# New constants in the ledger that paces an involution under an attention (VectorE and GpSimd charged by start-to-start intervals)

## The chip, the cores and the metric

The kernel runs on one core of one Trainium2 chip. The metric is the device time of one execution, in microseconds (us); lower is better. Engines are named as in the profile: PE (TensorE matmul), PEld (its weight loads), DVE (VectorE), ACT (ScalarE), POOL (GpSimd) and SP (the queue that issues most transfers).

## The reference

Four images x of 512 channels by 64 x 64 pixels in fp32 go through two layers.

```python
# layer 0: attention over the 4096 pixels of one image, 128 inner channels
q, k, v = wq @ xf + bq, wk @ xf + bk, wv @ xf + bv
attn = softmax(einsum('bci,bcj->bij', q, k), axis=-1)
x = wo @ einsum('bcj,bij->bci', v, attn) + bo + x
# layer 1: involution, 7 x 7 taps, 8 groups of 16 channels
o = relu(affine(W1 @ x))                  # 512 -> 128 channels
w = Ws @ relu(affine(Wr @ o)) + bs        # 49 x 8 weights for every pixel
out[g, c, h, w] = sum over taps of w[g, tap] * o_padded[g, c, shifted by tap]
x = affine(W3 @ out) + x                  # 128 -> 512 channels
```

The softmax is taken without a running maximum. A second, general path in the program runs only if a check on the row sums asks for it; it does not run on these inputs.

## The kernel before, in words

**Attention.** An image's 4096 pixels are eight chunks of 512. `keys_values` (L473) makes keys and values of an image, chunk by chunk. `attention` (L647) then goes through the query chunks; a chunk has 32 steps. A step m issues the score matmul `pss` of step m + 2, ACT's exponential into `pt` (five buffers), the output matmul `po` of step m, and DVE's addition of `pt` into `pacc`, whose column sums give the softmax's divisor. Each 512-column product is two instructions on PE. The last image's last chunk is done as two halves of 256 queries.

**Finishing a chunk.** `finish_block` (L520) is a generator with the rest of a chunk: the row sums (`blocks`, `pl`, `rls`, `spread`), the normalised output `on`, four `pwo` matmuls and updates of `x`, the 512-to-128 product `p`, its result `o`, a transpose of it that goes by DMA into a padded image in DRAM (`pix`), and the reduced channels `red`. A chunk holds two involution units; `units` lists those whose chunk is finished.

**Involution.** A unit is four image rows; an image has 16, numbered 0 to 15. `ring` holds windows of `pix` rows in SBUF, loaded by `pump` (L240) through SP. `involution` (L306) makes, per unit, the tap weights `pw` on PE (into a PSUM bank that the unit before has read), and then products `prod<-ring,pw` on DVE (L356), each over three or four tap lines (one or two where the ring wraps): 49 lines in 14 to 21 products. The first product of the unit goes straight into `acc`; the others go through four `prod` buffers and are added to `acc` by POOL (L380). Two folds on POOL (L389) end the unit. In the first three images `turn_unit` (L395) then transposes the unit with DVE (`turned`, L404) and DMAs (`turns`, `accT`); in the last image PE transposes it (L436). `close_chunk` (L454) makes four `py` matmuls, DVE's updates of `x`, and the store.

**What sets the order.** All this is written into one program in an order that a ledger decides while the program is built; no engine reads it at run time. `pe` is the time of all matmuls issued so far (0.86 us for 512 columns). `free["dve"]`, `free["pool"]` and `free["dma"]` say until when those are taken; `takes` (L176) books an operation:

```python
def takes(engine, us):
    free[engine] = max(free[engine], pe) + us
    return free[engine]
```

After some of its matmuls the attention calls `chores` (L269): one step of a finishing block, one of a closing, and `pace` (L232), which lets `involution` go on while it has credit (1.56 tap lines per us of `pe`, at most 20). A product is issued only when this does not hold:

```python
while not tail and (
    pe < max(begin, landed)
    or free["dve"] > pe + (4.5 if b == B - 1 else 3.5)
    or free["pool"] > pe + lag
):
    yield "wait"
free["pool"] = max(free["pool"], takes("dve", DVE_TAPS[0] + DVE_TAPS[1] * n))
takes("pool", POOL_TAPS[0] + POOL_TAPS[1] * n)
```

`lag` is 4.0 us while keys and values are made and 7.5 in the attention. The POOL line is booked for every product, the first of a unit too, for which POOL gets nothing. `DVE_OP` is booked for each addition of `pt` (L692) and for the 512-column steps of finishing and closing (L403, L460, L536 to L559, L603); 1.5 `POOL_OP` for a unit's two folds (L392). A unit begins when `pe` has reached `free["dve"]` + 0.3 (L313). `turn_unit` waits for POOL's booked end + 2.0; in the last image the finishing block waits twice for `free["dve"]` + 0.8 (`HOP_US`).

**The tail.** When the last image's attention is written, `tail` is set. From then on no wait of the ledger holds, and every second product of a unit is summed on PE, by multiplication with the identity (`pa<-ident,prod`), instead of on POOL.

A scheduler behind the program may reorder instructions on an engine; products inside the attention are pinned to their place.

Of the kernel before, what the change touches and what calls it, by code (L numbers as in the profile page):

```python
# [64 lines left out]


PE_COLUMN = 0.43 / 256
DVE_OP, POOL_OP = 0.7, 1.28
DVE_TAPS, POOL_TAPS = (0.16, 0.27), (0.19, 0.55)
ROW_US, X_US, PIX_US, LAND_US = 2.2, 3.8, 1.5, 3.0  # L70
HOP_US = 0.8
STEP_US = 1.0
# [1052 lines left out]
```

## Time and profile before

| what | before |
|---|---|
| time, median of 3 runs (lowest to highest) | 2606.61 us (2604.79 to 2607.39) |
| span of the profiled execution | 2605.7 us |
| PE busy | 2587.9 us, 99% |
| DVE busy | 1874.2 us, 72% |
| POOL busy | 1823.5 us, 70% |
| ACT busy | 835.8 us, 32% |
| POOL additions (L380) | 1063, 1701.5 us |
| DVE products into `prod` (L356) | 1092, 886.7 us |
| DVE additions into `pacc` (L696) | 958, 664.6 us |
| granted PE clock, mean | 0.997 |

The profile is one execution. Its span runs from the first to the last instruction, and no time of the whole execution is given beside it, so it is the profiled execution's own time here, 0.9 us below the median of the runs. A group's "mean" is the time between an instruction's start and its end in the record; the distance from one start to the next is read from the timeline, which lists start, duration, engine, line, operation, output and inputs, shape, count, and in brackets how long the engine was idle before and who ended that. The chain of waits follows the last instruction back to what released it. PE's instructions overlap, so that its rate too is read from starts.

Inside the attention the four images are nearly copies of each other: units 1 to 15 of image 1 and of image 2 start at the same distances to within 0.1 us.

### The profile page before, as it was taken

How to read it: one execution, taken by the hardware profiler on the slowest of the kernel's cores; microseconds unless marked ns; L12 is line 12 of the kernel's file. 1: busy time of each engine (PE TensorE's matmuls, PEld its weight loads, DVE VectorE, ACT ScalarE, POOL GpSimd, SP SyncE). 2: the span in 40 equal slices, each digit the busy share in tenths (PEclk: the TensorE clock that was granted, in tenths of full speed). 3: DMA queues.
4: the chain of work that ended last, by engine and by line, in shares of the span. 5: the costliest groups of instructions: out<-in, count | busy, mean ns of one | idle time of the engine just before them, and what ended most of it. 6: DMA issues, size and time to landing. Idle time of an engine off the chain costs nothing.

```text
span 2605.7 us, 24569 instructions
## 1 busy us (share of the span) xinstructions
PE 2587.9 (99%) x7484; PEld 1246.5 (48%) x7484; DVE 1874.2 (72%) x2677; ACT 835.8 (32%) x1378; POOL 1823.5 (70%) x1197
## 2 busy tenths in 40 slices
PE   9999999999999999999999999999999999999998
PEld 7444444445544444444644444444464444444577
DVE  0447777877575787788676678788757678777887
ACT  1333333332233333333223333333323333333330
POOL 0007788877881788887885468888788577877886
PEclk9999999999999999999999999999999999999999
DMA  6033232445615344233651434443463433222343
GB/s 236 1 75 63 55 85 73 99 99 150 164 43 112 63 101 95 61 84 82 180 129 45 103 69 101 101 92 74 118 171 83 101 93 93 72 60 58 73 91 102
DMA packets 208798, 244.33 MB, mean 94 GB/s; under 512 B 109640, under 2 KB 128528, under 8 KB 208528
## 3 DMA queue, kind: packets, MB, share of 16 engines
q1 hardware_dynamic: 208224, 242.31, 38.6%
q8 instruction: 61, 1.00, 0.2%
q14 instruction: 81, 0.66, 0.1%
q10 hardware_dynamic: 432, 0.36, 0.0%
HBM read 193.57 MB, written 49.06 MB: 93 GB/s over the span
## 4 chain that ended last, share of the span: by engine, by line
PE 91%; POOL 4%; DVE 3%; issue 1%; DMA 0%; ACT 0%; SPq 0%; POOLq 0%; DVEq 0%; ACTq 0%
PE pss L220 32%; PE po L220 31%; PE pv L220 4%; PE pk L220 4%; PE pq L220 4%; PE pwo L220 4%; PE py L220 4%; PE p L220 4%; POOL acc L380 4%; PE pw L220 2%; DVE prod L356 1%; PE pa L220 1%; DVE pacc L696 1%; PE pr L220 1%; POOL acc L389 0%
## 5 line engine op out<-in xcount | busy, mean ns | idle before, releaser
L380 POOL TENSOR_TENSOR acc<-acc,prod 128x768 f32<-128x768 f32 (+3 forms) x1063 | 1701.5, 1620 | 760.5 <-DVE prod L356 712.4
L220 PE MATMUL pss<-q,k 128*128 128x512 f32 (+1 forms) x2112 | 1056.3, 585 | 0.0
L220 PE MATMUL po<-pt,v 128*128 128x512 f32 (+1 forms) x2112 | 1047.7, 581 | 0.0
L665 ACT ACTIVATE pt<-pss 128x512 f32<-128x512 f32 x1024 | 611.3, 597 | 1252.0 <-PE pss L220 1184.9
L356 DVE TENSOR_TENSOR prod<-ring,pw 128x512 f32<-128x512 f32 (+3 forms) x1092 | 886.7, 847 | 44.6 <-POOL acc L380 41.7
L696 DVE TENSOR_TENSOR pacc<-pacc,pt 128x512 f32<-128x512 f32 x958 | 664.6, 694 | 243.2 <-ACT pt L665 216.2
L220 PEld LDWEIGHTS po<-pt,v 128*128 128x128 f32 x2112 | 399.3, 190 | 482.2 <-issue 462.2
L220 PEld LDWEIGHTS pss<-q,k 128*128 128x128 f32 x2112 | 391.9, 190 | 466.2 <-issue 459.3
L404 DVE STREAM_TRANSPOSE turned<-acc 128x256 f32<-128x256 f32 x48 | 21.4, 446 | 217.4 <-POOL acc L389 217.4
L220 PE MATMUL py<-accT,wt 128*128 128x512 f32 (+1 forms) x264 | 132.3, 584 | 4.0 <-DVE x L461 3.3
L220 PE MATMUL pwo<-on,wt 128*128 128x512 f32 (+1 forms) x264 | 130.3, 586 | 0.0
L220 PEld LDWEIGHTS pv<-wt,x 128*128 128x128 f32 x1024 | 119.6, 192 | 15.3 <-issue 15.0
L389 POOL TENSOR_TENSOR acc<-acc 128x512 f32<-128x512 f32 x120 | 119.5, 996 | 9.4
L461 DVE SCALAR_TENSOR_TENSOR x<-py,vec,x 128x512 f32<-128x512 f32 (+1 forms) x132 | 95.7, 726 | 36.1 <-PE py L220 35.8
L220 PE MATMUL pv<-wt,x 128*128 128x128 f32 x1024 | 120.2, 275 | 0.0
L220 PE MATMUL p<-x,wt 128*128 128x512 f32 (+1 forms) x264 | 119.2, 579 | 0.0
L578 ACT ACTIVATE x<-x,vec 128x512 f32<-128x512 f32 (+1 forms) x132 | 92.9, 706 | 80.0 <-PE p L220 74.9
L220 PE MATMUL pk<-x,wt 128*128 128x512 f32 x256 | 117.3, 596 | 0.1
L220 PE MATMUL pq<-x,wt 128*128 128x512 f32 (+1 forms) x264 | 115.4, 580 | 0.0
L560 DVE SCALAR_TENSOR_TENSOR x<-pwo,bo,x 128x512 f32<-128x512 f32 (+1 forms) x132 | 95.2, 727 | 22.8 <-PE pwo L220 21.7
L356 DVE TENSOR_TENSOR acc<-ring,pw 128x1024 f32<-128x1024 f32 (+1 forms) x84 | 78.7, 955 | 17.6 <-PE pw L220 17.6
L220 PEld LDWEIGHTS pq<-x,wt 128*128 128x128 f32 x264 | 50.0, 190 | 60.2 <-issue 56.7
(57 smaller groups left out, 733.6 us busy)
## 6 DMA issues: line engine op xcount, KB each, us to landing
x<-x_dram SPq DMA_DIRECT2D x55, 1024.0 KB, 5.7
ring<-pix SPq DMA_DIRECT2D x74, 448.0 KB, 8.3
ring<-pix SPq DMA_DIRECT2D x24, 1344.0 KB, 9.7
out_dram<-x SPq DMA_DIRECT2D x31, 1024.0 KB, 4.2
ring<-pix SPq DMA_DIRECT2D x24, 896.0 KB, 10.7
ring<-pix SPq DMA_DIRECT2D x30, 672.0 KB, 10.2
ring<-pix SPq DMA_DIRECT2D x6, 2240.0 KB, 19.5
pix<-o1t SPq DMA_DIRECT2D x192, 32.0 KB, 1.7
```

The source lines that it names most:

```text
L220: return nc.tensor.matmul(o, lhsT=lhsT, rhs=rhs, start=start, stop=stop)
L356: product = nc.vector.tensor_tensor(prod[:, :, p0 : p0 + n, :].rearrange("p t d (g c) -> p t d g c", g=G), image.rearrange("p t d (g c) -> ...
L380: nc.gpsimd.tensor_tensor(acc[:, :, d0 : d0 + n, :], acc[:, :, d0 : d0 + n, :], prod[:, :, :n, :], ALU.add,)
L389: nc.gpsimd.tensor_tensor(acc[:, :, :n, :], acc[:, :, :n, :], acc[:, :, n : 2 * n, :], ALU.add)
L404: nc.vector.transpose(blocks.rearrange("p (t k q) -> p t k q", t=NT, q=TB), acc[:, :, 0, :].rearrange("p t (k q) -> p t k q", q=TB),)
L461: nc.vector.scalar_tensor_tensor(xt[:, t, :], py, v1(V_S3 + t), xt[:, t, :], ALU.mult, ALU.add)
L560: nc.vector.scalar_tensor_tensor(xt[:, t, :], pw, bo[:, t : t + 1], xt[:, t, :], ALU.add, ALU.add)
L578: nc.scalar.activation(xt[:, t, :], xt[:, t, :], AF.Identity, bias=v1(V_B3 + t))
L665: nc.scalar.activation(pt, pss, AF.Exp)
L696: nc.vector.tensor_tensor(paccs[k], paccs[k], pt, ALU.add)
```

## The change

Five numbers of the ledger are replaced. `DVE_OP` and `POOL_OP` are the booked time of a 512-element operation on DVE and POOL. `DVE_TAPS` and `POOL_TAPS` are a fixed part and a part per tap line of a product and of its addition. The old numbers are near an instruction's duration, the new ones are meant as the time from one instruction's start to the next one's.

```diff
 PE_COLUMN = 0.43 / 256
-DVE_OP, POOL_OP = 0.7, 1.28
-DVE_TAPS, POOL_TAPS = (0.16, 0.27), (0.19, 0.55)
+DVE_OP, POOL_OP = 0.62, 1.23
+DVE_TAPS, POOL_TAPS = (0.065, 0.267), (0.14, 0.545)
 ROW_US, X_US, PIX_US, LAND_US = 2.2, 3.8, 1.5, 3.0
```

| booked, us | before | after |
|---|---|---|
| DVE, product of 4 / 3 / 2 / 1 lines | 1.24 / 0.97 / 0.70 / 0.43 | 1.133 / 0.866 / 0.599 / 0.332 |
| POOL, addition of 4 / 3 / 2 / 1 lines | 2.39 / 1.84 / 1.29 / 0.74 | 2.32 / 1.775 / 1.23 / 0.685 |
| DVE, addition of `pt` | 0.70 | 0.62 |
| POOL, a unit's folds | 1.92 | 1.845 |

No instruction is written differently. What changes is after which matmul a product, a unit's weights, a finishing or a closing step stands in the program, and so how much of the last image is left when `tail` is set.

## The prediction

> **What bounds the kernel now.** I read the page's engine shares first, then stretches of the span, then the waits, then rows of the timeline.
>
> ```profile
> span 2605.7 us, 24569 instructions
> PE 2587.9 (99%) x7484; PEld 1246.5 (48%) x7484; DVE 1874.2 (72%) x2677; ACT 835.8 (32%) x1378; POOL 1823.5 (70%) x1197
> ```
>
> TensorE (PE) is busy for all but 17.8 us. The table of stretches (busy us of PE, weight loads, DVE, ACT, POOL; then the granted clock) shows where those lie:
>
> ```profile
> 694.00:1247.00 553.00, 551.70 (x1332) 239.13 (x1331) 425.34 (x620) 187.76 (x309) 404.61 (x270) 1.00 0.37 84
> 1959.00:2525.00 566.00, 565.99 (x1555) 275.60 (x1554) 441.03 (x630) 200.58 (x338) 432.76 (x287) 1.00 0.34 80
> 2525.00:2606.00 81.00, 68.00 (x460) 57.34 (x458) 64.55 (x92) 4.97 (x12) 52.66 (x33) 0.93 0.36 94
> ```
>
> Image 1 leaves PE idle 1.3 of 553 us, the last image's attention nothing, and the tail (attention over, the involution's rest alone) 13 of 81. An earlier product can shorten only the tail; inside the attention it can only remove or make stalls.
>
> The waits (us in total, times, longest) say who waits for the paced work:
>
> ```profile
> POOL acc L380 <- DVE prod L356: 712.4, 157, 199.8
> DVE turned L404 <- POOL acc L389: 217.4, 48, 7.3
> DVE prod L356 <- POOL acc L380: 41.7, 76, 1.8
> ACT pt L665 <- DVE prod L356: 39.0, 31, 2.0
> ```
>
> The transposes `turned` hold DVE 4.5 us each, at most 7.3, and PE does not stop behind any: ACT is late 2.0 us at most, and the score matmul that needs ACT's buffer still starts 1.78 us or more after ACT's end around each of them.
>
> **The change, part by part.** No instruction is added or dropped in the attention; five constants of a ledger change. So the first question is how each constant stands to start-to-start times. Back-to-back rows of DVE's timeline (start, duration):
>
> ```profile
> 1486.99 0.69 DVE L696 TENSOR_TENSOR pacc<-pacc,pt 128x512 f32<-128x512 f32 x1
> 1487.59 0.94 DVE L356 TENSOR_TENSOR prod<-ring,pw 128x768 f32<-128x768 f32 x1
> 1488.45 0.69 DVE L696 TENSOR_TENSOR pacc<-pacc,pt 128x512 f32<-128x512 f32 x1
> 1489.05 0.94 DVE L356 TENSOR_TENSOR prod<-ring,pw 128x768 f32<-128x768 f32 x1
> ```
>
> An addition lasts 0.69 but the next starts 0.60 later; a three-line product lasts 0.94, next 0.86 later. Over all such pairs the medians are 0.33, 0.60, 0.86 and 1.13 us for one to four lines. The new DVE numbers (0.065 + 0.267n: 0.332, 0.599, 0.866, 1.133) are these; 0.62 lies between 0.60 (`pacc`) and 0.66 (the PSUM-reading `x` updates). POOL, from the chain (start, us):
>
> ```profile
> 341.69 1.82 POOL acc L380
> 343.59 1.83 POOL acc L380
> ...
> 355.54 2.38 POOL acc L380
> 357.99 2.37 POOL acc L380
> ```
>
> Three lines start 1.90 apart, four 2.45, so POOL's interval is longer than its duration there. The new POOL numbers (1.775 and 2.32) are 0.12 short, the old (1.84, 2.39) 0.06. But the ledger charges a unit for an addition that POOL never gets (the first product lands in acc directly). A whole unit (7 products of four lines, 7 of three), POOL: old 7×2.39 + 7×1.84 + 1.92 = 31.5, new 7×2.32 + 7×1.775 + 1.85 = 30.5, real 6×2.45 + 7×1.90 + 2.1 = 30.1. DVE: old 7×1.24 + 7×0.97 = 15.5, new 14.0, real 14.0. The ledger gets 1.0 us shorter per unit on POOL, 1.5 on DVE, and stays just above POOL's real time.
>
> The Trainium skill, "VectorE: DVE Perf Modes", section "The DRAIN you can't avoid", speaks against the change: it draws the next DVE operation as unable to issue until the pipe of the one before is empty. By that the old durations are right, the new ledger undercounts DVE by 1.5 us a unit, and the sum would gain a stall of about that size at many units; by the rows (0.60 between starts of 0.69) it gains none.
>
> *Pace inside the attention.* A step is a score and an output matmul of 512 columns, 0.86 us each, 1.72. A four-line product plus one addition was 1.24 + 0.70 = 1.94 on DVE's ledger, is now 1.75; a three-line one 1.67, now 1.49. DVE's limit (3.5 us ahead) then rarely holds a product, POOL's (7.5) does. The third limit, 1.56 lines per us, gives a unit's 49 lines in 31.4 us, while units start 36 us apart: it binds neither ledger. A unit closes 1 to 1.5 us earlier. Its cost on PE is nothing: PE's work is the same, and the last image, whose DVE limit of 4.5 lets POOL decide already, shows PE idle for 0.01 us in 566. DVE has the room (441 busy of 566).
>
> *What is queued behind it.* DVE meets `turned` up to 1.5 us sooner against a POOL that is no faster: its wait grows from 4.5 to some 6, the longest from 7.3 to 8.8. Behind it stand the `pacc` additions, behind them ACT's `pt` buffers (five), then PE. The cover is the 1.78 us that no wait up to 7.3 has touched: cost 0, at worst 8.8 − 7.3 − 1.78, below 0. If that cover were gone, 1.5 us in 48 places is 72.
>
> *PE's own waits on DVE at a unit's edge.* `pw` overwrites the bank that the last unit's last product reads. In image 1 its start lies 0.15, 0.91, 1.39, 1.78, 1.85 us after that product's end in the five tightest units, 2.7 and more elsewhere. And one place per image stalls already:
>
> ```profile
> 381.06 1.12 PE L220 MATMUL py<-accT,wt 128*128 128x512 f32 x2 [1.10 <-DVE x L461]
> 382.41 0.93 PE L220 MATMUL pw<-wt,red 33*128 33x392 f32 x4 [0.22 <-DVE prod L356]
> 383.27 2.07 PE L220 MATMUL pss<-q,k 128*128 128x512 f32 x2
> ```
>
> By start-to-start excess it costs 1.6 us, again at 1015 and 1648, and in image 0 another 1.8 because the clock was granted at half for 3.4 us (the pair in the last row: 2.07 for 1.02): 6.6 in all. Bounds: all gone, −6.6; moved 1.4 us tighter, (1.25 + 0.5) × 3 = +5.2; moved 2 us, 3.9 × 3 = +11.8. I take 0: the product closes earlier by 1.0 to 1.5 while the gate in front of `pw` (DVE's ledger plus 0.3) closes earlier by the same, so slacks scatter round what they are.
>
> *Finishing steps of the last image.* They wait for DVE's ledger plus 0.8. A ledger backlog of 4.5 us shrinks by 12%, 0.5 us. `pl` starts 2.7 us or more after its input, `pwo` 1.9 or more: hidden. The PE transposes of `acc` there start 4.8 us or more after POOL's end, so 1.0 earlier is hidden too. On SP's queue each unit's four `turns` transfers, every other unit's `accT` load and the ring loads behind them move by the 1 to 2 us of their unit; `accT` lands 14.9 us or more before `py` needs it, so that is hidden too, and a ring row sooner only helps; the ring rows that the last units need are set by the last finishing block, not by the ledger; POOL issues none.
>
> *The tail.* The last four units start here on DVE (first product of each; the third is split):
>
> ```profile
> 2513.86 1.22 DVE L356 TENSOR_TENSOR acc<-ring,pw 128x1024 f32<-128x1024 f32 x1 [2.13 <-PE pw L220]
> 2541.59 1.21 DVE L356 TENSOR_TENSOR acc<-ring,pw 128x1024 f32<-128x1024 f32 x1
> 2556.31 0.68 DVE L356 TENSOR_TENSOR acc<-ring,pw 128x512 f32<-128x512 f32 x1
> 2577.50 1.21 DVE L356 TENSOR_TENSOR acc<-ring,pw 128x1024 f32<-128x1024 f32 x1
> ```
>
> Unit 11 starts at 2477.6, 0.3 us after its rows' finishing step, so only units 11 and 12 add up: unit 12 starts 1.7 to 3.4 us (one or two steps) earlier, and one or two more of its products lie ahead of 2525. Each takes 1.13 us of DVE out of the tail, where DVE is the serial engine (65 of 81): −1.1 to −2.3, by POOL's 2.45 each −2.5 to −4.9. The ring rows of the third unit land at 2554.2, 2.1 us before its start, which caps the gain near 2.1. Other end: one product falls back, or one more goes to POOL: +2.4. I take −2.0.
>
> **Sum.** 2605.7 + 0 (attention) + 0 (edges) − 2.0 (tail) = 2603.7. The profiled span is 0.9 below the median 2606.6; with that, 2604.6.
>
> **Rivals.** *A, nothing that can be measured (forecast):* edges between −3 and +3, tail −2: 2602 to 2608. That the order barely changes (2606.6) is in it. For it: PE idle of 1.3 us per image, 0.01 in the image already in the new regime. *B, slower:* `pw` stands on PE ahead of the product that still reads its bank, and all matmuls queue behind it. It decides from 1.4 us of lost slack on (+5.2); at 2.0 it is +11.8, less the tail's 2.0: 2616. Against it: the gate moves with DVE's ledger, now exact. For it: DVE's delays behind POOL (41.7 us) are in no ledger, and a stall can bring the half clock, 1.8 us each. *C, faster:* the stalls at 381, 1015 and 1648 vanish (−6.6) and the tail gains 2 to 4: 2596 to 2598. For it: `py` there waits on a DVE step whose place the smaller numbers move; against: all three must go.
>
> **How the numbers follow.** 0.2% is 5.2 us, about what a measurement of this kernel can tell from no change. A 0.45, B 0.31, C 0.24. The likeliest case gives 2604.6, its own range 2602 to 2608. The 8-in-10 range leaves out B's far end (moved over 2 us or more clock losses) and C's: 2597 to 2617. Faster 0.24, same 0.45, slower 0.31.
>
> **What would show it.** Right: PE idle of 1.3 us or less per image; DVE's wait before `turned` some 1 us longer; POOL's idle between units longer, its busy time the same; unit 12's first product near 2511. Wrong: a new wait of PE (`pw` or `py` for DVE) repeated once per image, half-clock rows after it, ACT's `pt` waits above 2 us, or a tail (2525 to the end) that differs from 81 by more than 4.

## The result, and the profile after

The changed kernel takes 2634.2 us (2632.2 to 2641.5) against 2606.6 before: slower by 27.6 us, ratio 1.0111 with a 95% interval of 1.0098 to 1.0123. The forecast was 2604.6, so both the size and the sign were missed.

The profiled execution's span is 2632.3 us. The page's share lines, after:

```profile
span 2632.3 us, 24463 instructions
PE 2594.5 (99%) x7434; PEld 1244.0 (47%) x7434; DVE 1881.9 (71%) x2677; ACT 834.9 (32%) x1378; POOL 1830.4 (70%) x1202
```

Every engine is as busy as it was; PE's share still reads 99%. So the shares can't say where 26.6 us went. The table of stretches, cut at the first key matmul of each image and at the end of the attention, does (stretch, its length, then busy us of PE, weight loads, DVE, ACT and POOL; then the granted clock). Before, images 1 and 3 and the tail:

```profile
617.80:1250.30 632.50, 631.20 (x1714) 289.56 (x1713) 468.05 (x671) 205.45 (x336) 469.23 (x306) 1.00 0.41 97
1882.70:2526.20 643.50, 643.49 (x1934) 325.72 (x1933) 481.94 (x679) 217.74 (x364) 495.14 (x320) 1.00 0.38 92
2526.20:2605.70 79.50, 66.80 (x455) 56.27 (x453) 63.35 (x91) 4.97 (x12) 51.63 (x32) 0.93 0.37 95
```

After, images 1, 2 and 3 and the tail:

```profile
620.50:1262.50 642.00, 634.98 (x1713) 290.64 (x1712) 470.19 (x670) 205.34 (x336) 468.98 (x306) 0.99 0.40 96
1262.50:1904.20 641.70, 635.00 (x1713) 290.52 (x1712) 470.20 (x670) 205.35 (x336) 468.94 (x306) 0.99 0.40 96
1904.20:2561.10 656.90, 650.35 (x1941) 327.61 (x1939) 492.87 (x688) 217.14 (x365) 505.77 (x325) 0.99 0.37 91
2561.10:2632.30 71.20, 58.45 (x398) 49.38 (x398) 56.31 (x82) 4.95 (x12) 47.87 (x32) 0.96 0.33 93
```

Images 1 and 2 are 9.5 and 9.2 us longer than before (632.5 each), image 3 13.4 us (643.5), image 0 2.6 us (613.3 to 615.9). The tail is 8.2 us shorter (79.4 to 71.2). The sum is +34.7 − 8.2 + 0.1 = +26.6.

I took the distance from the start of each PE instruction to the next, less the usual distance for its shape, and put the excess under "stall" where PE was idle before the instruction and under "half clock" where it lies in a stretch with the clock granted at 0.5. That gives for images 0 to 3:

| us | stall, before | after | half clock, before | after |
|---|---|---|---|---|
| image 0 | 1.9 | 4.1 | 1.8 | 1.8 |
| image 1 | 1.6 | 7.6 | 0.0 | 3.6 |
| image 2 | 1.6 | 7.3 | 0.0 | 3.2 |
| image 3 | 0.2 | 7.0 | 0.0 | 3.5 |

So the stalls grow by 20.7 us and the half clock by 10.3; 2.5 us are matmuls of the tail that now stand in image 3; 1.2 us of the 34.7 are in none of these.

PE's own waits for DVE inside the images, after (us in total, times, longest; those of `pa`, in the tail, are left out); before, `py` for DVE was 3.3 and `pw` for DVE 0.7:

```profile
PE pw L220 <- DVE prod L356: 14.3, 6, 2.5
PE py L220 <- DVE x L461: 3.8, 3, 1.5
PE pwo L220 <- DVE x L560: 3.6, 1, 3.6
PE pq L220 <- DVE x L461: 2.2, 3, 0.7
```

In all four, PE waits for something that is late on DVE, although DVE is busy only 71% of the span. What DVE itself waits for, after:

```profile
DVE turned L404 <- POOL acc L389: 210.7, 45, 7.6
DVE prod L356 <- POOL acc L380: 65.4, 128, 1.5
```

The waits before `turned` are what they were (217.4 in 48), those for a free product buffer were 41.7 in 76. The timeline shows how the two come to PE. At 1388, DVE then PE (start, duration):

```profile
1379.98 1.50 DVE L696 TENSOR_TENSOR pacc<-pacc,pt 128x512 f32<-128x512 f32 x2
1386.93 0.45 DVE L404 STREAM_TRANSPOSE turned<-acc 128x256 f32<-128x256 f32 x1 [5.45 <-POOL acc L389]
1387.30 0.71 DVE L461 SCALAR_TENSOR_TENSOR x<-py,vec,x 128x512 f32<-128x512 f32 x1
```

```profile
1386.30 1.02 PE L220 MATMUL py<-accT,wt 128*128 128x512 f32 x2
1388.06 2.41 PE L220 MATMUL pq<-x,wt 128*128 128x512 f32 x5 [0.74 <-DVE x L461]
```

DVE stands 5.45 us before `turned`, the update of `x` that frees the PSUM bank for `pq` stands behind it, and PE waits. At 2063.9 `pwo` waits 3.6 us for an `x` behind a `turned` that stood 4.36; this `turned` is of image 2's last unit, which ends in image 3's stretch. At 1018.6 it is the other wait: between 1005 and 1013 five products on DVE had stood 1.28, 1.14, 0.93, 0.30 and 0.30 us for a buffer, the unit's last one ends at 1018.4, and `pw`, which overwrites what that product reads, starts 2.5 us late, with the clock halved right behind it (a pair of 512 columns 2.08 us long, 1.02 elsewhere):

```profile
1015.04 1.02 PE L220 MATMUL po<-pt,v 128*128 128x512 f32 x2
1018.60 1.01 PE L220 MATMUL pw<-wt,red 33*128 33x392 f32 x4 [2.54 <-DVE prod L356]
1019.54 2.08 PE L220 MATMUL pss<-q,k 128*128 128x512 f32 x2
```

Three of the six waits of `pw` are of this kind, in front of unit 5 of images 0 to 2. The other three, in front of unit 15, have a `turned` behind them that ended long before:

```profile
1352.19 0.45 DVE L404 STREAM_TRANSPOSE turned<-acc 128x256 f32<-128x256 f32 x1 [4.13 <-POOL acc L389]
1378.25 1.81 DVE L356 TENSOR_TENSOR prod<-ring,pw 128x768 f32<-128x768 f32 x2
1380.21 0.93 PE L220 MATMUL pw<-wt,red 33*128 33x392 f32 x4 [2.26 <-DVE prod L356]
```

From this `turned` to the end of the product at 1380.1 are 27 us, and DVE is idle for 0.87 us of them: it has not made up the 4.13 us that it stood when PE comes to `pw`. The run with `turned` held, further down, tests this.

### The profile page after: what moved, and what is told of

It reads as the page before. It is cut to its first block, busy times and chain, and to the rows that moved or that the text cites. A ratio compares the mean times of both kernels' runs of the same rounds, so it can differ in the third digit from the quotient of the medians.

```text
span 2632.3 us, 24463 instructions
## 1 busy us (share of the span) xinstructions
PE 2594.5 (99%) x7434; PEld 1244.0 (47%) x7434; DVE 1881.9 (71%) x2677; ACT 834.9 (32%) x1378; POOL 1830.4 (70%) x1202
## 5 line engine op out<-in xcount | busy, mean ns | idle before, releaser
L356 DVE TENSOR_TENSOR prod<-ring,pw 128x512 f32<-128x512 f32 (+3 forms) x1092 | 891.4, 850 | 83.2 <-POOL acc L380 65.4
L404 DVE STREAM_TRANSPOSE turned<-acc 128x256 f32<-128x256 f32 x48 | 21.4, 445 | 210.7 <-POOL acc L389 210.7
L560 DVE SCALAR_TENSOR_TENSOR x<-pwo,bo,x 128x512 f32<-128x512 f32 (+1 forms) x132 | 95.1, 728 | 21.4 <-PE pwo L220 20.2
L220 PEld LDWEIGHTS pwo<-on,wt 128*128 128x128 f32 x264 | 50.1, 193 | 60.6 <-issue 48.8
## 6 DMA issues: line engine op xcount, KB each, us to landing
ring<-pix SPq DMA_DIRECT2D x24, 896.0 KB, 13.4
ring<-pix SPq DMA_DIRECT2D x32, 672.0 KB, 10.9
```

The costliest lines, as they stand in the source:

```text
L220: return nc.tensor.matmul(o, lhsT=lhsT, rhs=rhs, start=start, stop=stop)
L356: product = nc.vector.tensor_tensor(prod[:, :, p0 : p0 + n, :].rearrange("p t d (g c) -> p t d g c", g=G), image.rearrange("p t d (g c) -> ...
L404: nc.vector.transpose(blocks.rearrange("p (t k q) -> p t k q", t=NT, q=TB), acc[:, :, 0, :].rearrange("p t (k q) -> p t k q", q=TB),)
L560: nc.vector.scalar_tensor_tensor(xt[:, t, :], pw, bo[:, t : t + 1], xt[:, t, :], ALU.add, ALU.add)
```

## The experiments

Three theories stood against each other. Theory 1: the gate before `pw` opens on a DVE ledger that is too early. Theory 2: both ledgers pack the products too densely for DVE. Theory 3, formed after the first runs: DVE's waits for POOL, which no ledger books, hold up what PE needs; the new numbers only move PE's needs behind them. "Before" is the median of the runs of the kernel before that share a chip with each experiment, 2605.8 to 2606.3 us.

### One half of the numbers at a time

```diff
-DVE_OP, POOL_OP = 0.7, 1.28
-DVE_TAPS, POOL_TAPS = (0.16, 0.27), (0.19, 0.55)
+DVE_OP, POOL_OP = 0.62, 1.28
+DVE_TAPS, POOL_TAPS = (0.065, 0.267), (0.19, 0.55)
```

> The kernel before with only the DVE numbers of the change (0.62; 0.065 + 0.267n); POOL's stay old. Theory 1 (the weight matmuls pw are let onto PE when DVE's ledger says the last product is done, and the real DVE is later, so PE stands and its clock is halved): the gate hangs on DVE's ledger, so this half alone brings most of the loss inside the images: +15 to +30 us over before, with PE waiting for DVE in pw 8 us or more in total. Theory 2 (it is the denser packing of products by both ledgers that makes DVE late): about half of the change's loss, +8 to +14.

Measured: 2610.4 us, 1.0016 (1.0007 to 1.0026), +4 us. In its profile (an execution 3 us shorter than the median) the images are 10.2 us longer than before and the tail 10.4 us shorter; `py` and `pwo` waits make 9.7 us, `pw` 1.5, and no half clock falls into the images.

```diff
-DVE_OP, POOL_OP = 0.7, 1.28
-DVE_TAPS, POOL_TAPS = (0.16, 0.27), (0.19, 0.55)
+DVE_OP, POOL_OP = 0.7, 1.23
+DVE_TAPS, POOL_TAPS = (0.16, 0.27), (0.14, 0.545)
```

> The kernel before with only the POOL numbers of the change (1.23; 0.14 + 0.545n); DVE's stay old. Theory 1: the gate of pw does not move, total -3 to +5 us over before, PE waiting for DVE in pw under 3 us in total. Theory 2: the POOL ledger is now 0.12 us short of an addition's interval, products meet full buffers, DVE is late: +8 to +14.

Measured: 2610.9 us, 1.0018 (1.0009 to 1.0028), +5 us; PE's waits in `pw` 5.4 us, the buffer waits 65.8.

Neither theory's sizes hold: the halves give +4 and +5, the whole +28. DVE's half lies in neither range; POOL's half lies in theory 1's, but its waits in `pw` do not. A product is let go only when both ledgers allow it, so each half leaves the other old gate standing; that would make the effects more than add up, though no run tests it by itself. The buffer waits are POOL's half alone (65.8 with it, 40.8 without), and by themselves they are cheap: the kernel with POOL's half has as many as the changed one (65.4) and loses 5 us.

### The gate before the weights

On the changed kernel:

```diff
-            yield from until(free["dve"] + 0.3)
+            yield from until(free["dve"] + 2.8)
```

> The changed kernel with the gate in front of a unit's weights opened at DVE's ledger plus 2.8 us in place of plus 0.3. Theory 1: PE's waits in pw (14.3 us in total) fall under 4 and the half-clock stretches inside the images from 7 to 3 or fewer; the images lose 20 us of their 35; total -5 to +12 us over before, as units start later too. Theory 2: DVE is late whatever the gate: total within 8 us of the changed kernel's +27.

Measured: 2631.9 us, 1.0101 (1.0084 to 1.0118). PE's waits in `pw` are still 13.5 us, the longest 3.2, and `py` makes 9.5. The stretches at half clock inside the images fall from 7 to 3 (one of them twice as long), as theory 1 said, and `pwo` waits 0.2 us in place of 3.6; but the images keep 28.2 of their 34.7 us. A gate 2.5 us later moved the stalls more than it cured them: theory 1's remedy fails.

On the kernel before, the other way:

```diff
-            yield from until(free["dve"] + 0.3)
+            yield from until(free["dve"] - 2.2)
```

> The kernel before, old numbers, with the gate in front of a unit's weights opened 2.5 us sooner (DVE's ledger minus 2.2 in place of plus 0.3). It puts a price on a weight matmul that comes too early, apart from the new numbers. Theory 1 (pw on a bank that DVE still reads): the tight units of images 0 to 2 (0.15, 0.9, 1.4, 1.8, 1.85 us of slack) go short by some 6 us per image, PE's waits in pw rise from 0.7 to 12 us or more, half-clock stretches follow, total +12 to +30 over before. If a waiting pw costs nothing beyond itself or the slack is not lost: 0 to +5.

Measured: 2626.9 us, 1.0080 (1.0063 to 1.0097), +20.7 us, with `pw` waits of 9.9 us, `pwo` 6.4, `py` 4.2. With the old numbers a `pw` that comes 2.5 us early costs three quarters of what the change did. So a place that is a step or two too early is enough; but `pw`'s waits miss the 12 us of theory 1, and the others are as large, which it does not say.

### DVE's waits for POOL

First the buffers alone, on the changed kernel; the order of instructions on every engine is the same as without:

```diff
-    prods = pool("prods", 4)
+    prods = pool("prods", 6)
```

> The changed kernel with six product buffers in place of four; the order on every engine is the same, so only DVE's waits for POOL can differ (65.4 us in 128 waits). If those waits are what makes DVE later than its ledger: they fall under 15 us, PE's waits in pw fall from 14.3 to under 5 and the total to +3 to +12 us over before. If DVE is late for the steps that stand ahead of the last product (pacc, x updates, turned): total stays at +20 to +27.

Measured: 2626.8 us, 1.0080 (1.0063 to 1.0097), 7.4 us below the changed kernel. The buffer waits fall to 12.3 us and `pw`'s to 5.1, about as expected (under 5) of the buffers as `pw`'s cause; but `pq` now waits 10.7 us and `py` 7.8 for updates of `x`. The total stayed at the other branch's +20: the larger part of the cause was left.

Then the transpose. In the program `turned` is written when the ledger has POOL's end 2 us behind it; counted in `pacc` additions, the scheduler had moved it 1 to 7 steps ahead on DVE in 13 of image 1's 16 units after the change (14 before it; two end among keys and values, where no step counts). In the one unit left it kept its place, and waited 0.0 us. Holding it behind the DVE instruction written before it, on the changed kernel (in the traces PE, ACT and POOL then have the order of the changed kernel, and DVE too but for `turned` and a few neighbouring `pacc` additions and updates of `x`):

```diff
-            nc.vector.transpose(
+            turned = nc.vector.transpose(
...
             )
+            tc.keep_in_program_order(turned)
```

> The changed kernel with the transpose turned held behind the DVE instruction written before it; the scheduler had moved it 1 to 7 steps ahead, where it waits for POOL. Theory 3 (the updates of x and the last products that PE needs stand on DVE behind turned or right after it): DVE's waits for POOL before turned fall from 211 us to under 40, PE's waits for DVE in py, pq and pwo from 9.6 to under 3 and in pw from 14.3 to under 9; total +5 to +15 over before. Theory 2 (products packed too densely): turned does not matter, total +22 to +28.

Measured: 2605.4 us, 0.9994 (0.9985 to 1.0004): the loss in total is gone, with the five new numbers as they are. In the images 8.1 of the 34.7 us are left; the tail, 7.7 us shorter than before, pays for them. The waits of DVE in this run:

```profile
DVE prod L356 <- POOL acc L380: 53.8, 100, 2.0
DVE turned L404 <- POOL acc L389: 10.6, 6, 2.6
```

and those of PE (the held kernels have one line more, so that L560 is L561):

```profile
PE pw L220 <- DVE prod L356: 5.2, 3, 1.7
PE pwo L220 <- DVE x L561: 0.8, 1, 0.8
```

`turned` costs DVE 10.6 us in place of 210.7, `py` and `pq` wait no more, `pw` a third of what it did: its three waits in front of unit 15 are gone, the three in front of unit 5, behind the buffers, are left. Theory 3 said +5 to +15 over before; the hold gave back more than that.

Both together:

```diff
-    prods = pool("prods", 4)
+    prods = pool("prods", 6)
...
+            tc.keep_in_program_order(turned)
```

> The changed kernel with turned held behind and six product buffers, both of DVE's waits for POOL taken away. If DVE's waits for POOL, which no ledger books, are the whole cause: PE's waits for DVE inside the images fall from 27 us to under 5, no half clock inside the images, and what stays is the shorter tail: 2595 to 2604 us. If packing counts: above 2612.

Measured: 2594.9 us, 0.9954 (0.9937 to 0.9970), 11.3 us faster than before. Its stretches:

```profile
614.00:1245.00 631.00, 631.00 (x1714) 289.61 (x1712) 471.00 (x671) 205.27 (x336) 468.68 (x305) 1.00 0.41 98
1245.00:1876.00 631.00, 631.00 (x1714) 289.64 (x1713) 471.10 (x671) 205.26 (x336) 468.69 (x305) 1.00 0.41 97
1876.00:2523.00 647.00, 646.18 (x1938) 326.28 (x1937) 488.64 (x687) 217.07 (x364) 503.60 (x324) 1.00 0.37 91
2523.00:2594.00 71.00, 59.27 (x402) 50.62 (x400) 55.98 (x83) 4.95 (x12) 48.49 (x32) 0.94 0.33 94
```

PE is never idle in images 1 and 2, its clock is whole in all four images, an image takes 631.0 us against 642 after the change, and the tail (69.9 us) stays as short as the change made it.

### The short POOL ledger

```diff
-DVE_TAPS, POOL_TAPS = (0.065, 0.267), (0.14, 0.545)
+DVE_TAPS, POOL_TAPS = (0.065, 0.267), (0.06, 0.595)
```

> The changed kernel with POOL's numbers for a product's addition at the measured intervals of three and four lines (0.06 + 0.595n: 1.845 and 2.44 in place of 1.775 and 2.32). If the loss comes from POOL's ledger being 0.12 us short per addition: DVE's waits for full buffers fall from 65 to under 48 us and the total to +3 to +12 over before. If not: +20 or more.

Measured: 2612.1 us, 1.0022 (1.0012 to 1.0032): +5.9, with buffer waits of 39.5 us and `pw` at 2.1. POOL's new numbers fit one and two lines and miss three and four by 0.12 us; put right, most of the loss in total is gone too. But the images are still 16.3 us longer than before, against 34.7, and a tail 10.9 us shorter hides it. For three and four lines these numbers are also nearly the old ones (1.84 and 2.39), so this run is close to the one with DVE's half alone, which took 2610.4; it is no separate proof that the 0.12 us is what did it. `py` and `pwo` still wait 4.6 and 4.9 us: the scheduler still moves `turned` ahead, and it waits 212.9 us.

### What the numbers are worth without the waits

The kernel before, old numbers, with the transpose held:

```diff
+            tc.keep_in_program_order(turned)
```

> The kernel before, old numbers, with turned held behind the DVE instruction written before it. Theory 3 (DVE's unbooked waits for POOL are what makes PE stop; the old numbers only happened to keep PE's needs away from them): DVE's waits for POOL before turned fall from 217 us to under 40 and with them the stall of py, one per image; the time falls by 3 to 6 us only, 2600 to 2604, as there is little to cure. If the hold itself is worth some 20 us whatever the numbers, as it was in the changed kernel: 2585 to 2592.

Measured: 2611.3 us, 1.0019 (1.0010 to 1.0029): slower by 5.5 us. Images 1 and 2 do lose their stalls (631.1 us each, 1.4 less), and `turned` waits 1.7 us; but in image 3 `pl` now waits 5.1 us for the row sums, with the clock at half for 10.2 us behind it. Both branches missed: the hold alone is no gain. The loss in image 3 comes from the other of DVE's waits for POOL. There the scheduler has also put some 60 of PE's 7484 instructions elsewhere, and the row sums stand on DVE behind five products that waited 1.48, 0.81, 1.47, 0.93 and 0.93 us for a buffer.

The same with six buffers:

```diff
-    prods = pool("prods", 4)
+    prods = pool("prods", 6)
...
+            tc.keep_in_program_order(turned)
```

> The kernel before, old numbers, with turned held and six product buffers: the partner of the changed kernel with both. The difference of the two is the change without DVE's waits for POOL. If the new numbers are then worth the shorter tail they brought (8 us less tail against 3 us of work moved ahead of it): this one takes 2599 to 2603 against 2594.9. If they are worth nothing: 2593 to 2597.

Measured: 2602.3 us, 0.9985 (0.9976 to 0.9995), as the first branch said. With PE's order the same as with four buffers, `pl` waits 1.3 us in place of 5.1, and no half clock falls into the images. Against 2594.9 with the new numbers, the change is worth −7.4 us once DVE's waits are away (−7.8 when each is set against the kernel before on its own chip): the tail is 77.0 here and 69.9 there.

The changed kernel with both, and POOL's numbers put right:

```diff
-DVE_TAPS, POOL_TAPS = (0.065, 0.267), (0.14, 0.545)
+DVE_TAPS, POOL_TAPS = (0.065, 0.267), (0.06, 0.595)
...
-    prods = pool("prods", 4)
+    prods = pool("prods", 6)
...
+            tc.keep_in_program_order(turned)
```

> The changed kernel with turned held, six product buffers, and POOL's numbers at the measured intervals (0.06 + 0.595n). With no waits of DVE left the 0.12 us per addition should matter no more: 2593 to 2598, like the same without it (2594.9). If POOL's short ledger still costs: 2588 to 2592.

Measured: 2593.1 us, 0.9946 (0.9929 to 0.9963), the fastest of all, 12.7 us below its runs of before. The difference to 2594.9 is inside both intervals, so POOL's 0.12 us no longer shows.

## Why the prediction was wrong, point by point

- **The constants against the intervals.** Right as far as it went: DVE's numbers are its starts, POOL's short by 0.12 us. Wrong in what followed. I compared whole units (30.5 booked, 30.1 real) and called the ledger sound; but the surplus is an addition booked for the first product, and in between the ledger runs short by 0.12 us with each addition of three or four lines. The buffer waits rose from 41.7 to 65.4 us, and with POOL's half alone they did the same. That half cost only 5 us, though: the short numbers are a part of the loss, not its whole.
- **"A unit closes 1 to 1.5 us earlier."** Mis-sized. Written out for both kernels, `pw` stands 0 to 3 steps of 1.72 us earlier in images 0 to 2 (3 steps in units 3, 5 and 15) and up to 8 in image 3. Units hand their start on to the next and steps are whole, so a microsecond per unit does not stay one.
- **"PE's own waits on DVE at a unit's edge", taken at 0.** This is the step that failed. I argued that the product and its gate close earlier by the same amount. They did not: in image 1 `pw` stands 3 steps earlier in units 3, 5 and 15, and its distance to the end of the product went from 3.3 to 0.25 us in unit 3, from 6.8 us to a wait of 2.3 in unit 15, and from a wait of 0.2 to one of 2.5 in unit 5. DVE stands for POOL in front of the product, which the ledger does not book; held `turned` and six buffers together took these waits to nothing. I had written DVE's delays behind POOL down as what speaks for rival B, and gave it 0.31. Its far end, +11.8 us, counted `pw` alone and 2 us of lost slack; the images lost 34.7, of it 20.7 stalls in `pw`, `py`, `pq` and `pwo` and 10.3 half clock.
- **"What is queued behind it", cost 0.** I followed only the `pacc` additions behind `turned`, to ACT's buffers and the 1.78 us in front of the scores; that cover held. I left out the updates of `x` that stand on DVE behind `turned` as well and free the banks for `py`, `pwo` and `pq`, and that DVE can stay late for some 27 us behind one such wait, up to the product that `pw` needs. These are the paths by which holding `turned` gave 28.8 us back. My reading that PE stops behind no `turned` was wrong for the kernel before too: with `turned` held and the old numbers, the stall of `py` once per image is gone. The longer wait that I named (4.5 to 6 us) did not come: it is 4.7 in the mean. Its place moved, not its length.
- **"Finishing steps of the last image", hidden.** `pl` keeps 1.65 us or more, but `pwo`, which started 1.9 to 5.0 us after its input in image 3's full chunks, now starts 0.06 to 2.7 us after it, and one `pwo` waits 3.6 us for a bank.
- **"The last image, whose DVE limit of 4.5 lets POOL decide already."** It was a poor precedent: for that image's own units `turned` does not exist, PE transposes instead, so the wait that matters is hardly in it. Only image 2's last units bring it there.
- **The tail, −2.0.** Right in sign, mis-sized: −8.2, of which 2.5 is work moved into image 3. Unit 12 starts 23.9 us ahead of the attention's end in place of 12.3, not 1.7 to 3.4 us sooner; the ring's landing did not cap it.
- **What would show it wrong.** A PE wait for DVE in `pw` repeated once per image with half clock behind it: seen as written.

The Trainium skill's rule ("VectorE: DVE Perf Modes", "The DRAIN you can't avoid") that I weighed against the change would have had its sign. The same section adds that a next operation that is not held starts earlier, which I left out. Its drawing is not what happened here: after the change, as before it, an addition or product starts some 0.08 us ahead of the recorded end of the one before, and the change gains 7.4 us when DVE's waits for POOL are out of the way.

What stays open: why those places, and not others, meet a late DVE is settled only unit by unit by the order that ledger and scheduler write. I show that the waits are needed for the loss, not that any other set of numbers would lose. Nor did any run try a ledger that books the waits.

## What to carry to other kernels

A ledger that paces an in-order queue should know what the queue waits for, not only what it executes: charging less for its operations while it knows no waits can take away the slack that paid for them, as it did here. Where the busiest engine is at 99%, look at each thing it needs from another engine and ask what stands in front of that there; one wait of 5 us on an engine that is 71% busy is harmless until a step that PE needs lands behind it, and that can be 27 us later. Remove the wait first (place of the waiting instruction, number of buffers), then tighten the numbers: in that order the same five constants gained 7.4 us, in the other they cost 27.6.

## What the runs showed of the hardware that was not expected

Half clock can follow a short idle time of PE. Over all thirteen profiled executions, inside the attention and counting idle times of 0.6 us and more: under 1.6 us, 1 of 54 was met by a stretch at half clock starting close to it; 1.7 to 2.0 us, 4 of 9; 2.2 to 2.6 us, 11 of 14; over 3 us, 8 of 9. These are all of the 24 stretches at half clock there. A stretch lasted 3.4 us or a multiple of it (6.8, 10.2), and cost about 1.8 us per 3.4. So the price of a stall here jumps at about 2 us, and between 1.7 and 2.6 us its length alone does not settle it. The Trainium skill ("TensorE: Matmul & The Clock Gate", "What's actually happening") puts the clock down to a free-running window of 3.4 us and half clock after at least one idle window; the length agrees, while 2.2 us of idle was mostly enough here.

POOL's addition starts 0.08 us after the recorded end of the one before for three and four lines (1.89 and 2.44 apart, 1.81 and 2.36 long), but before it for one and two lines (0.69 and 1.23 apart, 0.73 and 1.28 long). A straight line through the short forms misses the long ones.
